# Sixteen heads of eight: 64 rows a head, the maxima inside the score pass, halves through DRAM, and unread matmuls

## The chip, the core and the metric

The kernel runs on one core of a Trainium2 chip. The metric is device microseconds of one execution, as the median of several runs. Engines work from queues of their own: TensorE (PE in the profile, with weight loads under PEld), VectorE (DVE), ScalarE (ACT), GpSimd (POOL) and SyncE (SP), which issues most DMAs.

## The reference

Four transformer layers follow one another on x of shape (16, 256, 128), each with an adaptive layer norm before an attention and before a feed-forward part. Two places matter here. Inside layer 1's feed-forward part there is a full attention with 16 heads of 8 dimensions, and layer 2's attention is a causal one with 16 heads of 8 dimensions and rotary positions:

```python
# layer 1, inner attention
q = (src @ Wq + bq).reshape(B, T, NHEAD, HEAD_DIM)      # NHEAD 16, HEAD_DIM 8, the same for k and v
scores = jnp.einsum('bqhd,bkhd->bhqk', q, k) * scale
probs = jax.nn.softmax(scores, axis=-1)
out = jnp.einsum('bhqk,bkhd->bqhd', probs, v).reshape(B, T, d)
# layer 2, attention
Q, K = rope((x @ qw).reshape(...)), rope((x @ kw).reshape(...))
score = Q @ jnp.swapaxes(K, -1, -2) / jnp.sqrt(jnp.float16(dim))   # masked below the diagonal, softmax
```

T is 256, so each batch row has a 256 x 256 score matrix for each of 16 heads, in both places.

## The kernel before

Activations lie transposed, 128 features on the partitions and 4096 tokens along the free axis, in 8 blocks of 512 tokens (two batch rows each). The stages run one after another: layer 0 attention, layer 0 experts, layer 1 attention, layer 1 inner attention (**stage A** here), layer 1 experts, layer 2 attention (**stage B**), layer 2 experts, layer 3. Stages A and B both run `attend8`, with `spaces8` for their buffers.

**Operands.** q and k are each split into a high and a low part (`parts8`), so that four products high-high, high-low, low-high, low-low add up to the score. `spread8` lays them out by 16 DMAs a block, from SBUF to SBUF: each head gets 32 partition rows (8 dimensions x 4 products), four heads fill 128 partitions, and four such groups c lie side by side. One matmul with 32 rows then gives one head's scores. A stage has 16 units of work, one for each batch row; two units make a block.

**Two passes over the scores.** The first pass computes scores with queries on the partitions, and DVE reduces them to row maxima (L1394). The second pass computes them again with keys on the partitions, subtracts the maxima in the same accumulation by an extra matmul (`pick8` times `mT`, the maxima split into two parts and transposed), and ACT takes the exponential (L1399). `less_maxima` makes `mT`. In stage B a mask is added in the first pass by two bf16 matmuls (`ident16` times `below`), and POOL clears the upper triangle after the exponential (L1402).

**Cycles.** A unit has 8 cycles. A cycle holds four first-pass matmuls of one unit and, `LEAD` + 8 = 10 cycles behind, the eight second-pass matmuls (four scores, four maxima) of an earlier tile; they are interleaved in the order of `steps[0] + steps[1]`. First-pass scores go to `ps_max` and second-pass ones to `ps_exp`, one buffer of two banks each. After them come the things put off from the cycle before (`held`): the maxima's transposes, the values, and `weighted`, which multiplies the exponentials by the values in four column groups of 32. Generators (`sides`, `ready`, `self.later`) add one step each per cycle: the norm and projection of the next block, leaving transposes, output projection, gates. TensorE's instructions keep the program's order (`strict`); other engines' are ordered by a scheduler.

```python
first = [(c, t, j0) for t in range(2) for c in range(2) for j0 in (2, 0)]
...
for o, lhsT, rhs, fresh in steps[0] + steps[1]:
    self.mm(o, lhsT, rhs, start=fresh, skip_group_check=True)
```

Of the kernel before, what the change touches and what calls it, by code (L numbers as in the profile page):

```python
# [20 lines left out]
P = 128  # L21
B, T = 16, 256
NT = B * T
BLK = 512
# [24 lines left out]
def _constants():  # L49
# [19 lines left out]
    put("pick", ((i[:, None] % 32 < 8) & (i[:, None] % 4 == np.arange(4)[None, :])).astype(np.float32))  # L69
# [154 lines left out]
class _Kernel:  # L224
# [825 lines left out]
    def layer1_attn(self):  # L1050
# [4 lines left out]
        with ExitStack() as ctx:  # L1055
# [67 lines left out]
            self.wi = self.load("i1_w", self.w, tag="small")  # L1123

            def inner():
# [4 lines left out]
                self.first_parts = self.w.tile([P, 2, 2, BLK], F32R, tag="m3", name="first_parts")  # L1130
                for _ in self.projected8(self.wi, hb, self.first_parts):
                    yield True

# [37 lines left out]
    LEAD = 2  # L1171

    def spaces8(self, pool, nt, ctx):
# [8 lines left out]
        for n in range(2):  # L1182
# [38 lines left out]
    def spread8(self, parts):  # L1221

        out = self.att.tile([P, 2, 4, BLK], F32R, tag="q8", name="q8")
        src = parts.bitcast(F32).rearrange("p a h t -> p (a h) t")
        for s in range(4):
            of_q, of_k = s // 2, 2 + s % 2
            for c in range(4):
                self.nc.sync.dma_start(
                    out=out.bitcast(F32)[s::4, :, c, :],
                    in_=src[32 * c : 32 * c + 32, of_q : of_k + 1 : of_k - of_q, :],  # L1230
                )
        return [out[:, a] for a in range(2)]

    def unit8(self, qk, hb, at, tok, wv, bias):
        q, k = (x[:, :, tok] for x in qk)
        self.units8.append(dict(q=q, k=k, hb=hb[:, tok], wv=wv, dst=at[:, tok], bias=bias, whole=(hb, at)))

    def attend8(self, group, prepare, finish, scale, causal=False, qmask=None):
# [6 lines left out]
        first = [(c, t, j0) for t in range(2) for c in range(2) for j0 in (2, 0)]  # L1245
# [955 lines left out]
```

## Time and profile before

| what | value |
|---|---|
| median of 6 runs (lowest, highest) | 3223.69 us (3217.08, 3239.49) |
| the profiled execution: its own time, its span | 3231.36 us, 3229.7 us |
| mean granted TensorE clock | 0.899 |
| busy: PE, PEld, DVE, ACT, POOL | 2847.5, 1820.6, 1920.3, 1701.4, 1331.0 us |
| stage A, first maxima matmul to last exponential | 1662.8 to 2049.1 us |
| stage B, the same | 2261.4 to 2730.8 us |
| first-pass reduction L1394 (246 from `ps_max`) | mean 1088 ns |
| exponential L1399 (256) | mean 915 ns |
| `spread8` DMAs | 256 of 128 KB |

The span is the time from the first to the last instruction of the profiled execution. The granted clock is the share of TensorE's clock that was let through. PE's busy time includes time in which matmuls wait in the pipeline, so it is not a measure of how full the array is.

### The profile page before, as it was taken

The page shows a single profiled execution, that of the slowest core. Times are in us where ns is not written, and L with a number is a line of the kernel's source. Part 1 is how long each engine was busy: PE and PEld are TensorE (multiplying, and loading weights), DVE is VectorE, ACT ScalarE, POOL GpSimd, SP SyncE. Part 2 cuts the span into 40 slices and gives each one's busy share as a digit, 9 for nine tenths or more (in the row PEclk, how much of TensorE's full clock was granted, in tenths as well). Part 3 has the DMA queues.
Part 4 walks back from the last instruction along what each step waited for, and adds up shares of the span by engine and source line. Part 5 has one row for each costly group of instructions (what it writes and reads, how often), then busy time and mean ns, then how long its engine had stood idle before and what let it go on. Part 6 is the DMA issues. An engine that isn't in the chain of part 4 may idle for free. (4 is left out here: it accounts for less than half of the span.)

```text
span 3229.7 us, 53104 instructions
## 1 busy us (share of the span) xinstructions
PE 2847.5 (88%) x19238; PEld 1820.6 (56%) x19238; DVE 1920.3 (59%) x4639; ACT 1701.4 (53%) x4484; POOL 1331.0 (41%) x1168
## 2 busy tenths in 40 slices
PE   6999999888979999999969999866789899999777
PEld 3566656555966677776644455564445555555433
DVE  4777777786535666666656666312555563645564
ACT  3777676565435566666625554433243433665533
POOL 4766777772134534443320012233432321333455
PEclk9999999999989999999978877778677776999998
DMA  8050000001752000000021122264212120000000
GB/s 301 2 53 1 9 6 6 11 19 48 225 151 65 14 3 1 1 1 1 1 53 43 43 61 66 71 178 111 51 47 52 27 53 1 1 1 1 4 11 13
DMA packets 87349, 146.14 MB, mean 45 GB/s; under 512 B 14240, under 2 KB 43104, under 8 KB 86832
## 3 DMA queue, kind: packets, MB, share of 16 engines
q1 hardware_dynamic: 65328, 112.98, 13.1%
q0 software_dynamic: 8512, 17.71, 1.9%
q10 hardware_dynamic: 13248, 12.06, 1.1%
q8 instruction: 153, 2.51, 0.3%
q14 instruction: 108, 0.88, 0.1%
HBM read 69.79 MB, written 43.54 MB: 35 GB/s over the span
## 5 line engine op out<-in xcount | busy, mean ns | idle before, releaser
L216 POOL TENSOR_TENSOR E<-E,sm_inv 128x1024 f32<-128x1024 f32 (+1 forms) x241 | 408.0, 1693 | 404.1 <-PE ps_big L259 173.1
L1399 ACT ACTIVATE E<-ps_exp 128x1024 f32<-128x1024 f32 (+1 forms) x256 | 234.2, 915 | 276.6 <-PE ps_exp L259 257.7
L1394 DVE TENSOR_REDUCE m<-ps_max 128x4 f32<-128x1024 f32 (+1 forms) x246 | 267.6, 1088 | 170.3 <-PE ps_max L259 165.4
L216 ACT ACTIVATE E<-E,sm_neg 128x256 f32<-128x256 f32 x512 | 254.1, 497 | 211.8 <-DVE sm_neg L1093 205.0
L216 POOL DMA_INDIRECT rows<-list_rows,l_i x128 | 128.2, 1001 | 497.3 <-ACT list_rows L216 309.7
L262 PEld LDWEIGHTS ps_one<-w_cst,E 128*128 128x128 f32 x1792 | 205.4, 142 | 174.9 <-POOL E L216 98.7
L262 PE MATMUL ps_one<-w_cst,E 128*128 128x128 f32 x1792 | 246.0, 277 | 53.4 <-POOL E L216 35.9
L216 DVE COPY PT<-ps_one 128x512 f32<-128x512 f32 x320 | 209.0, 685 | 96.6 <-PE ps_one L262 94.3
L259 PE MATMUL ps_big<-kT,qT 64*128 64x256 f32 (+1 forms) x2048 | 265.5, 378 | 0.0
L259 PE MATMUL ps_one<-PT,v 128*64 128x256 f32 (+1 forms) x2048 | 225.0, 362 | 3.0 <-DVE PT L216 2.7
L216 ACT ACTIVATE E<-ps_big,sm_neg 128x128 f32<-128x128 f32 (+1 forms) x512 | 208.9, 423 | 25.4 <-DVE sm_inv L216 19.8
L216 POOL TENSOR_TENSOR r_r<-r_r,r_t 128x512 f32<-128x512 f32 x128 | 162.7, 1271 | 137.5 <-DVE r_t L216 120.6
L259 PE MATMUL ps_exp<-q 32*128 32x256 f32 (+1 forms) x1064 | 199.3, 388 | 20.7 <-ACT E L1399 17.5
L1093 DVE CUSTOM_DVE_ANT_0 E<-ps_big,bias 128x256 f32<-128x256 f32 x512 | 186.7, 421 | 51.1 <-PE ps_big L259 24.5
L259 PE MATMUL ps_max<-q 32*128 32x256 f32 (+1 forms) x984 | 158.4, 396 | 51.5 <-DVE m L1394 25.6
L259 PEld LDWEIGHTS ps_big<-kT,qT 64*128 64x128 f32 x2048 | 166.7, 187 | 58.2 <-issue 49.5
L216 POOL DMA_INDIRECT list_rows<-done,origin x128 | 123.2, 963 | 182.5 <-DVE acc L216 41.7
L259 PE MATMUL ps_out<-E,v 128*32 128x256 f32 (+1 forms) x2048 | 191.1, 451 | 3.1 <-POOL E L1402 2.8
L259 PEld LDWEIGHTS ps_max<-q 32*128 32x128 f32 x984 | 97.7, 234 | 150.2 <-issue 73.1
L1402 POOL TENSOR_SCALAR_AFFINE_SELECT E<-E 128x512 f32<-128x512 f32 x128 | 83.0, 650 | 234.5 <-ACT E L1399 234.5
L259 PEld LDWEIGHTS ps_one<-PT,v 128*64 128x64 f32 x2048 | 132.5, 138 | 80.4 <-DVE sm_inv L216 13.6
L259 PE MATMUL ps_exp<-mT,pick 32*128 32x256 f32 (+1 forms) x1024 | 163.4, 329 | 0.0
(351 smaller groups left out, 6460.1 us busy)
## 6 DMA issues: line engine op xcount, KB each, us to landing
q<-parts SPq DMA_DIRECT2D x240, 128.0 KB
rows<-zeros SPq DMA_DIRECT2D x8, 2048.0 KB
list_w<-in_f_W SPq DMA_DIRECT2D x46, 257.0 KB
done<-l_o ACTq DMA_DIRECT2D x92, 128.0 KB
f_W<-in_f_W SPq DMA_DIRECT2D x27, 386.0 KB
f_room<-in_f_W SPq DMA_DIRECT2D x19, 386.0 KB
list_sums<-rows SPq DMA_DIRECT2D x46, 128.0 KB
rb_rows<-rb_d SPq DMA_DIRECT2D x1, 4088.0 KB
```

Source lines behind the costliest of these rows:

```text
L216: ins = f(*args, **kw)
L259: self.ordered(self.nc.tensor.matmul(out, lhsT, rhs, start=start, stop=stop, **kw))
L262: self.ordered(self.nc.tensor.transpose(out, in_, self.c("ident")))
L1093: nc.vector.tensor_tensor_reduce(e[:, i], S[:, i], bias[g][:, i, off : off + T], 1.0, BIG, ALU.add, ALU.min, neg[:, i : i + 1])
L1394: nc.vector.tensor_reduce(o, Sm[:, :, :, :nk], AX.X, ALU.max, negate=True)
L1399: nc.scalar.activation(E, Se[:, :, :, q0:], AF.Exp, scale=scale)
L1402: nc.gpsimd.affine_select(D, D, [[0, 4], [1, P]], ALU.is_ge, 0.0, base=0, channel_multiplier=-1)
```

## The change

- **64 rows a head.** `spread8` gives each head 64 partition rows: row 64 h + 8 d + s for dimension d and product s = 0 to 3. Rows with s = 4 to 7 are zero in q; in k the rows 62 and 63 of each head are one (constant `last`). Two heads fill the partitions and eight groups lie side by side. First-pass matmuls read 60 rows, second-pass ones 64.
- **The maxima in the score pass.** The negated maxima, high and low part, are written by four small DMAs a unit into rows 62 and 63 of q, so the second pass needs no extra matmul. A cycle has 8 score matmuls in place of 12, all of the first pass ahead of the second.
- **Halves through DRAM.** The parts are stored to DRAM by one DMA a block (`stored8`), and each unit is spread from there by 8 DMAs into one of three standing buffers (`q8`, initialised in `spaces8` by DVE, POOL and ACT), called when the unit before the unit before begins its second pass.
- **Unread matmuls.** `turning` issues bf16 matmuls of the identity with itself, 512 columns each, whose result nothing reads: 20 where each stage begins, 2 in each cycle before the second pass has begun, and, in stage A alone, one in each cycle, into the `ps_exp` buffer ahead of the second-pass scores.
- `LEAD` becomes 3, and `weighted` runs for each cycle's own tile, one cycle after it.

```diff
-    put("pick", ((i[:, None] % 32 < 8) & (i[:, None] % 4 == np.arange(4)[None, :])).astype(np.float32))
+    put("last", (i[:, None] % 64 >= 62).astype(np.float32))
...
-    LEAD = 2
+    LEAD = 3
...
             self.v8.append(v)
-            m = pool.tile([P, nt, 4, 4], F32, tag=f"m8_{n}", name=f"m8_{n}")
-            r = pool.tile([P, nt, 4, 32], F32R, tag=f"r8_{n}", name=f"r8_{n}")
-            nc.vector.tensor_copy(r, bc(self.zero.unsqueeze(2).unsqueeze(3), [P, nt, 4, 32]))
+            m = pool.tile([P, nt, 2, 8], F32, tag=f"m8_{n}", name=f"m8_{n}")
+            r = pool.tile([P, nt, 2, 16], F32R, tag=f"r8_{n}", name=f"r8_{n}")
             self.m8.append((m, r))
-        self.pick8 = pool.tile([P, 4, P], F32R, tag="pick8", name="pick8")
-        nc.vector.tensor_copy(self.pick8, bc(self.c("pick").unsqueeze(2), [P, 4, P]))
+        self.q8 = []
+        for n in range(3):
+            q = pool.tile([P, 2, 8, nt * P], F32R, tag=f"q8_{n}", name=f"q8_{n}")
+            shape = [P, 8, nt * P]
+            (nc.gpsimd if n else nc.vector).tensor_copy(q[:, 0], bc(self.zero.unsqueeze(2), shape))
+            nc.scalar.copy(q[:, 1], bc(self.c("last").unsqueeze(2), shape))
+            self.q8.append(q)
...
-    def spread8(self, parts):
-
-        out = self.att.tile([P, 2, 4, BLK], F32R, tag="q8", name="q8")
-        src = parts.bitcast(F32).rearrange("p a h t -> p (a h) t")
+    def stored8(self, parts):
+
+        out = self.parts8_dram.tile([P, 4, BLK], F32, tag="parts", name="parts8")
+        self.nc.sync.dma_start(out=out, in_=parts.bitcast(F32).rearrange("p a h t -> p (a h) t"))
+        return out
+
+    def turning(self, ps, n):
+
+        for _ in range(n):
+            self.mm(ps, self.ident16, bc(self.ident16.unsqueeze(1), [P, 4, P]), skip_group_check=True)
+
+    def spread8(self, u):
+
+        d = self.units8[u]
+        parts, tok = d["parts"]
+        out = self.q8[u % 3]
+        src = parts.rearrange("(c r) x t -> r c x t", r=16)
         for s in range(4):
-            of_q, of_k = s // 2, 2 + s % 2
-            for c in range(4):
-                self.nc.sync.dma_start(
-                    out=out.bitcast(F32)[s::4, :, c, :],
-                    in_=src[32 * c : 32 * c + 32, of_q : of_k + 1 : of_k - of_q, :],
-                )
-        return [out[:, a] for a in range(2)]
-
-    def unit8(self, qk, hb, at, tok, wv, bias):
-        q, k = (x[:, :, tok] for x in qk)
-        self.units8.append(dict(q=q, k=k, hb=hb[:, tok], wv=wv, dst=at[:, tok], bias=bias, whole=(hb, at)))
+            for a, of in enumerate((s // 2, 2 + s % 2)):
+                self.nc.sync.dma_start(out=out.bitcast(F32)[s::8, a], in_=src[:, :, of, tok])
+        d["q"], d["k"] = out[:, 0], out[:, 1]
+
+    def unit8(self, parts, hb, at, tok, wv, bias):
+        self.units8.append(dict(parts=(parts, tok), hb=hb[:, tok], wv=wv, dst=at[:, tok], bias=bias, whole=(hb, at)))
...
         NQ = nt * P
-        first = [(c, t, j0) for t in range(2) for c in range(2) for j0 in (2, 0)]
+        first = [(c, t) for t in range(2) for c in range(4)]
         if causal:
-            then = [(c, t, j0) for t in (1, 0) for c in range(2) for j0 in (0, 2)]
+            then = [(c, t) for t in (1, 0) for c in range(4)]
         else:
-            then = [(c, t, j0) for c in range(2) for t in range(2) for j0 in (0, 2)]
+            then = [(c, t) for c in range(4) for t in range(2)]
...
@@ -1265,23 +1279,31 @@
             while step(g):
                 pass
+        def spread(u):
+            if u % group == 0 and u // group in ready:
+                run(ready.pop(u // group))
+            self.spread8(u)
+
         def start_unit(u):
             blk, i = divmod(u, group)
-            if i == 0:
-                run(ready.pop(blk))
-                if blk + 1 < NBLK:
-                    ready[blk + 1] = prepare(blk + 1)
+            if i == 0 and blk + 1 < NBLK:
+                ready[blk + 1] = prepare(blk + 1)
         def less_maxima(u):
             m, r = self.m8[u % 2]
-            hi = r[:, :, :, :4]
+            hi = r[:, :, 0]
+            m = m.rearrange("p t j c -> p t (j c)")
             nc.vector.tensor_copy(hi, m)
-            nc.vector.tensor_sub(r[:, :, :, 4:8], m, hi.bitcast(F32))
-            ps = self.bank()[:, :NQ]
+            nc.vector.tensor_sub(r[:, :, 1], m, hi.bitcast(F32))
+            ps = self.bank()[:32, :NQ]
             for t in range(nt):
-                self.turned(ps[:, t * P : (t + 1) * P], r[:, t].bitcast(F32).rearrange("p j x -> p (j x)"))
-            mT = U[u]["mT"] = self.att.tile([P, NQ], F32R, tag="mT", name="mT")
+                self.turned(ps[:, t * P : (t + 1) * P], r[:, t].bitcast(F32).rearrange("p s x -> p (s x)"))
+            mT = self.att.tile([32, NQ], F32, tag="mT", name="mT")
             nc.vector.tensor_copy(mT, ps)
+            q = U[u]["q"].bitcast(F32)
+            for n in range(4):
+                row = 64 * (n % 2) + 62 + n // 2
+                nc.sync.dma_start(out=q[row : row + 1], in_=mT[8 * n : 8 * n + 8, :])
...
-        def weighted(u, x, E, i):
+        def weighted(u, x, E):
             d = U[u]
-            c, t, _ = then[x]
+            C, t = then[x]
+            c, i = divmod(C, 2)
             q0 = t * P if causal else 0
-            if i == 0 and t == then[0][1]:
+            fresh = t == then[0][1] and i == 0
+            if fresh:
                 out = self.ps_out.tile([P, 512], F32, tag="out", name="ps_out")
                 d["out", c] = out.rearrange("p (i q) -> p i q", i=2)
             out = d["out", c]
             for j in range(4):
                 self.mm(
                     out[32 * j : 32 * j + 32, i, q0:],
-                    self.v8[u % 2][:, t, 8 * c + 4 * i + j, :],
-                    E[:, j, i, q0:],
-                    start=t == then[0][1] and i == 0,
+                    self.v8[u % 2][:, t, 4 * C + j, :],
+                    E[:, j % 2, j // 2, q0:],
+                    start=fresh,
                     stop=t == then[-1][1],
                     skip_group_check=True,
                 )
             if i == 0:
-
-                held.append(lambda: weighted(u, x, E, 1))
                 return
...
             if mx == 0:
+                run(ready.pop(0))
+                spread(0)
                 start_unit(0)
-            steps = [[], []]
+                spread(1)
+                self.turning(self.ps_out.tile([P, 512], F32, tag="out", name="ps_out"), 20)
+            if live_e and et == 0 and eu + 2 < units:
+                spread(eu + 2)
             if live_m:
-                c, t, j0 = first[mt]
+                c, t = first[mt]
                 nk = (t + 1) * P if causal else NQ
                 d = U[mu]
                 if live_e or mx % 2 == 0:
@@ -1366,39 +1393,38 @@
                 else:
                     Sm = self.ps_exp.tile([P, 1024], F32, tag="exp", name="ps_exp")
-                Sm = Sm.rearrange("p (j i k) -> p j i k", j=2, i=2)
+                Sm = Sm.rearrange("p (r n k) -> p r n k", r=2, n=2)
+                if not live_e:
+                    self.turning(self.ps_out.tile([P, 512], F32, tag="out", name="ps_out"), 2)
                 if qmask is not None:
-                    for j in range(2):
-                        self.mm(Sm[:, j, :, nk - P : nk], self.ident16, bc(qmask.unsqueeze(1), [P, 2, P]), skip_group_check=True)
-                for i in range(2):
-                    for j in range(2):
-                        r = slice(32 * (j0 + j), 32 * (j0 + j) + 32)
-                        q, k = d["q"][r, 2 * c + i, t * P : (t + 1) * P], d["k"][r, 2 * c + i, :nk]
-                        steps[i].append((Sm[:, j, i, :nk], q, k, qmask is None and i == 0))
+                    for r in range(2):
+                        self.mm(Sm[:, r, :, nk - P : nk], self.ident16, bc(qmask.unsqueeze(1), [P, 2, P]), skip_group_check=True)
+                for n in range(2):
+                    for r in range(2):
+                        rows = slice(64 * r, 64 * r + 60)
+                        q, k = d["q"][rows, 2 * c + n, t * P : (t + 1) * P], d["k"][rows, 2 * c + n, :nk]
+                        self.mm(Sm[:, r, n, :nk], q, k, start=qmask is None and n == 0, skip_group_check=True)
             if live_e:
-                xc, xt, xj0 = then[et]
+                xc, xt = then[et]
                 q0 = xt * P if causal else 0
                 e = U[eu]
-                Se = self.ps_exp.tile([P, 1024], F32, tag="exp", name="ps_exp").rearrange("p (j i q) -> p j i q", j=2, i=2)
-                for i in range(2):
-                    rows = [slice(32 * (xj0 + j), 32 * (xj0 + j) + 32) for j in range(2)]
-                    for j, r in enumerate(rows):
-                        k, q = e["k"][r, 2 * xc + i, xt * P : (xt + 1) * P], e["q"][r, 2 * xc + i, q0:]
-                        steps[i].append((Se[:, j, i, q0:], k, q, i == 0))
-                    for j, r in enumerate(rows):
-                        steps[i].append((Se[:, j, i, q0:], self.pick8[r, 2 * xc + i, :], e["mT"][r, q0:], False))
-            for o, lhsT, rhs, fresh in steps[0] + steps[1]:
-                self.mm(o, lhsT, rhs, start=fresh, skip_group_check=True)
+                Se = self.ps_exp.tile([P, 1024], F32, tag="exp", name="ps_exp")
+                if qmask is None:
+                    self.turning(Se[:, :512], 1)
+                Se = Se.rearrange("p (r n q) -> p r n q", r=2, n=2)
+                for n in range(2):
+                    for r in range(2):
...
+                        self.mm(Se[:, r, n, q0:], k, q, start=n == 0, skip_group_check=True)
             if live_m:
-                o = self.m8[mu % 2][0][:, t, j0 : j0 + 2, 2 * c : 2 * c + 2]
+                o = self.m8[mu % 2][0][:, t, :, 2 * c : 2 * c + 2]
                 nc.vector.tensor_reduce(o, Sm[:, :, :, :nk], AX.X, ALU.max, negate=True)
             if live_e:
-                if xj0 == 0:
-                    e["E"] = self.att.tile([P, 4, 2, NQ], F32, tag="E8", name="E8", bufs=3)
-                E = e["E"][:, xj0 : xj0 + 2, :, q0:]
-                nc.scalar.activation(E, Se[:, :, :, q0:], AF.Exp, scale=scale)
+                E = self.att.tile([P, 2, 2, NQ], F32, tag="E8", name="E8", bufs=3)
+                nc.scalar.activation(E[:, :, :, q0:], Se[:, :, :, q0:], AF.Exp, scale=scale)
                 if causal:
-                    D = e["E"][:, xj0 : xj0 + 2, :, q0 : q0 + P].rearrange("p j i q -> p (j i) q")
+                    D = E[:, :, :, q0 : q0 + P].rearrange("p r n q -> p (r n) q")
                     nc.gpsimd.affine_select(D, D, [[0, 4], [1, P]], ALU.is_ge, 0.0, base=0, channel_multiplier=-1)
             now, held = held, []
             for f in now:
@@ -1407,8 +1433,8 @@
                 held.append(lambda u=mu: less_maxima(u))
             if live_e and et == 0:
                 held.append(lambda u=eu: values(u))
-            if live_e and xj0 == 2:
-                held.append(lambda u=eu, x=et, E=e["E"]: weighted(u, x, E, 0))
+            if live_e:
+                held.append(lambda u=eu, x=et, E=E: weighted(u, x, E))
             sides = [g for g in sides if step(g)]
```

More of the change, by code (lines that the diff above doesn't have):

```diff
@@ L1123, in layer1_attn @@
             self.wi = self.load("i1_w", self.w, tag="small")
+            self.parts8_dram = self.pool("parts8", 3, DRAM)
             def inner():
@@ L1129, in inner @@
                     yield True
-                self.first_parts = self.w.tile([P, 2, 2, BLK], F32R, tag="m3", name="first_parts")
-                for _ in self.projected8(self.wi, hb, self.first_parts):
+                parts = self.w.tile([P, 2, 2, BLK], F32R, tag="m3", name="first_parts")
+                for _ in self.projected8(self.wi, hb, parts):
                     yield True
+                self.first_parts = self.stored8(parts)
             D[0] = {}
@@ L1390, in attend8 @@
-            for o, lhsT, rhs, fresh in steps[0] + steps[1]:
-                self.mm(o, lhsT, rhs, start=fresh, skip_group_check=True)
+                Se = self.ps_exp.tile([P, 1024], F32, tag="exp", name="ps_exp")
[4 more added lines that the diff above has]
+                    for r in range(2):
+                        rows = slice(64 * r, 64 * r + 64)
+                        k, q = e["k"][rows, 2 * xc + n, xt * P : (xt + 1) * P], e["q"][rows, 2 * xc + n, q0:]
+                        self.mm(Se[:, r, n, q0:], k, q, start=n == 0, skip_group_check=True)
@@ L1495, in prepare @@
                         yield from self.projected8(wi, hb, parts)
+                        parts = self.stored8(parts)
                     else:
                         hb, parts = self.h1, self.first_parts
-                    qk = self.spread8(parts)
-                    yield
                     at = two.tile([P, BLK], F32, tag="at", name="at", bufs=3)
                     for i in range(2):
-                        self.unit8(qk, hb, at, slice(i * T, (i + 1) * T), wi[:, 2 * P : 3 * P], self.v("i1_bv"))
+                        self.unit8(parts, hb, at, slice(i * T, (i + 1) * T), wi[:, 2 * P : 3 * P], self.v("i1_bv"))
                 def finish(blk, hb, at):
@@ L1701, in prepare @@
                 yield from self.turned8(w, hb, parts)
-                qk = self.spread8(parts)
-                yield
+                parts = self.stored8(parts)
                 at = two.tile([P, BLK], F32, tag="at", name="at", bufs=3)
                 for i in range(2):
-                    self.unit8(qk, hb, at, slice(i * T, (i + 1) * T), w[:, 4 * P : 5 * P], None)
+                    self.unit8(parts, hb, at, slice(i * T, (i + 1) * T), w[:, 4 * P : 5 * P], None)
             def finish(blk, hb, at):
```

## The prediction

> **What bounds the kernel now.** I read the page, then windows cut at the stages, then single 3.41-us stretches, then the timeline of one cycle and of the two stage starts. The page:
>
> ```profile
> span 3229.7 us, 53104 instructions
> PE 2847.5 (88%) x19238; PEld 1820.6 (56%) x19238; DVE 1920.3 (59%) x4639; ACT 1701.4 (53%) x4484; POOL 1331.0 (41%) x1168
> PEclk9999999999989999999978877778677776999998
> ```
>
> The granted clock sags from stage A to the end of stage B, and hardly elsewhere. The windows (busy of PE, PEld, DVE, ACT, POOL, then granted clock) are A's start, A's steady part, what lies between, B's start, B's steady part:
>
> ```profile
> 1662.80:1686.90 24.10, 14.50 (x56) 5.99 (x56) 15.82 (x19) 3.32 (x5) 0.00 (x0) 0.50 0.20 50
> 1686.90:2049.10 362.20, 332.05 (x2974) 184.23 (x2976) 230.25 (x445) 194.69 (x270) 46.90 (x48) 0.79 0.20 52
> 2049.10:2246.60 197.50, 145.37 (x784) 118.05 (x781) 53.38 (x160) 70.16 (x163) 61.59 (x68) 0.79 0.48 136
> 2246.60:2293.60 47.00, 27.91 (x110) 14.25 (x109) 19.32 (x34) 6.84 (x11) 16.97 (x16) 0.64 0.27 68
> 2293.60:2730.80 437.20, 390.94 (x3222) 223.28 (x3222) 235.99 (x447) 170.78 (x279) 133.69 (x172) 0.74 0.15 39
> ```
>
> PE is busy over 89% of both steady parts, no other engine over 64%. At full clock a plain cycle repeats in 1.85 us, paced by the reduction (1.22) and the exponential (1.02) taking turns with PE; at half clock it takes 2.34, paced by PE.
>
> ```profile
> 1708.54 1.22 DVE L1394 TENSOR_REDUCE m<-ps_max 128x4 f32<-128x1024 f32 x1 [1.06 <-PE ps_max L259]
> 1708.81 1.02 ACT L1399 ACTIVATE E<-ps_exp 128x1024 f32<-128x1024 f32 x1 [0.89 <-PE ps_exp L259]
> ```
>
> So the question is what sets the clock. It changes only at boundaries 3.41 us apart, and a busy PE does not bring it back:
>
> ```profile
> 1899.89:1903.30 3.41, 2.57 (x27) 1.31 (x24) 2.70 (x4) 1.35 (x2) 0.00 (x0) 0.50 0.02 5
> 1903.30:1906.71 3.41, 3.41 (x32) 2.29 (x32) 1.38 (x2) 1.02 (x1) 0.00 (x0) 0.50 0.68 160
> 1906.71:1910.13 3.42, 3.42 (x26) 2.06 (x24) 1.32 (x2) 2.04 (x4) 0.00 (x0) 0.50 0.78 195
> ```
>
> What fits is the amount of array streamed. For every matmul I counted its columns times the share of the 128 x 128 array that it uses, over each stretch. At full clock 58 of 61 stretches under 3000 such columns are followed by half clock, and 1 of 664 at 3000 or more; at half clock 53 of 59 at 3000 or more are followed by full clock, and 6 of 127 under it. [...]
>
> **What the change does to that count.** Before, a cycle of A streams 12 x 256 x 1/4 = 768 columns of scores and maxima and 1024 of `weighted`: 1792. After, 8 x 256 x 1/2 = 1024, 512 of turning, 1024: 2560. B gets no turning; its mean cycle goes from 1856 to 2048. I put these weights on the trace's own timing. Of A's stretches, 10 of 62 at full and 32 of 44 at half clock are under 3000 now; after, none and 5. Of B's, 16 of 60 and 51 of 68 now; after, 13 and 30. A should hold full clock; B should in part.
>
> **Stage A, steady (362).** Adding the full-clock period of each of the 16 cycle places in a block (1.84 to 5.02 us) gives 39.6 us; eight blocks are 317, with 8 of the experts' list work that rides along, 325: -37. Against it: matmul pairs start 0.11 us apart, and a cycle loses two pairs (-0.22) but gains a turning (512 columns at the 0.11 us per 256, +0.21) and two changes between full-array and part-array matmuls. Before shows such a change at B's mask:
>
> ```profile
> 2445.93 0.38 PE L259 MATMUL ps_max<-half_below,ident 128*128 128x256 bf16 x2
> 2446.24 0.33 PE L259 MATMUL ps_max<-q 32*128 32x128 f32 x2
> ```
>
> The second bf16 matmul starts 0.11 after the first, the next kind 0.20 after that: 0.09 a change. Net +0.17 a cycle. Nine places are plain ones paced by DVE and ACT, whose waits hide it; the other seven pay: 0.17 x 7 x 8 = +10. [...]
>
> **Starts.** A's 16 DMAs (10.5 us of issue) are followed by the first maxima:
>
> ```profile
> 1651.91 10.54 SPq L1228 DMA_DIRECT2D q<-first_parts  x16
> 1662.82 0.58 PE L259 MATMUL ps_max<-q 32*128 32x256 f32 x2 [11.05 <-DMA q<-first_parts]
> ```
>
> After, the parts were stored earlier, in the experts' time, so only 8 DMAs (8 x 0.65 + 2.2 landing = 7.4) stand ahead of the first unit, but three `q8` buffers are filled first: DVE 2.3, ACT 1.9 each (by 0.69 for 512 and 1.02 for 1024 elements). POOL fills two halves, 5.1 each by its 1.27 for 512, needed only by units 1 and 2. -1 (-5 to +4). The 20 turnings run in this gap and hide, 20 x 0.43 at half clock = 8.5 of 11 us. A's lead, 24.1 us at 0.50, becomes 11 cycles at the faster rate: -3 (-6 to +2). In B the store is new on the path: parts are ready at 2252.3; a 1 MB store lands about 5.5 later by this trace's stores, then 7.4 of spreads: 2265 against 2261.4, +4 (+2 to +8). B's turnings come as soon as `ident16` is there, near 2247, so the clock has fallen again: lead -1 (-5 to +4). Filling B's buffers falls into A's drain, where ACT copies `at`: +1.
>
> **Stage B, steady (437).** Full-clock periods add up to 45.2 a block, 372 in all with the blocks' tail work: -65 if the clock were always full. The count says that half-clock stretches go from 68 to about 25, because the 13 that still fall each last near two: -40 (-65 to 0). The score slot of a cycle shortens with two pairs gone, 0.57 to 0.43 in causal sizes, in the 7 PE-paced places: -8. `weighted` now takes each cycle's own exponential after POOL's clearing (650 ns, 127 in B), where every second one had a cycle more; `held` puts it one cycle later, so a cycle of 1.85 covers 0.65 unless POOL is in a 1.27-us `rot` or `parts` step (24 of them). Before, PE waited for it only 7.6 us. +6 (0 to +20).
>
> **Late maxima.** Rows 62 and 63 now come by DMA: transposes and copies 2.3 us, four issues on SP at 0.33 to 0.65, landing 2.2: 5.8 to 7.1 us after the unit's last reduction is under way. Three cycles of LEAD give 3 x 1.85 + 0.45 = 6.0 in A's odd units, 7 in B's, 10 and more in even ones. On SP they stand behind up to 8 spreads (5.2) and the store, which is itself queued until its parts are complete; whoever waits is the second pass, and behind it in PE's order the first pass and `weighted` of every later cycle. SP has 16 spreads, 8 row DMAs and a store a block, 12.9 us of issue against 30 and more. A: +6 (0 to +12). B: +2 (0 to +8).
>
> **Sum.** A: -1 - 3 - 37 + 10 + 6 = -25. B: +4 - 1 - 40 - 8 + 6 + 2 = -37. Elsewhere +1. Together -61. The profiled execution took 3231.4 (span 3229.7 and 1.7 around it), 7.7 above the median of 3223.7: 3170.4 there, 3163 as a median.
>
> **The rivals.**
> *Only A gains.* B gets no turning, and if its stretches stay under 3000, because faster stretches are also emptier in the 3.6 to 5.4 us cycles, the -40 goes: -25 + 3 + 1 = -21, 3203. For it: 13 full stretches still fall by my count. Against: 51 low half stretches become 30. Chance 0.22.
>
> *Slower: the clock does not follow.* The monitor may not weigh 64-row or unread matmuls as I do; no row before has either. Then A stays near 0.79, and turning is pure cost: +0.17 in seven of 16 places at full (75 cycles, +6), +0.35 in each of 52 half-clock cycles (+18), lead +5, late maxima +6, start -1: +34; B +3, elsewhere +1: +38, 3262. It decides if A's steady clock stays under 0.85. Against: the bf16 mask matmuls and the transposes are counted by the same rule and fit it. Chance 0.14.
>
> *Late maxima.* If the row DMAs land 1.5 us later than I take, because they queue behind the spreads, every unit of 32 stalls that much more: +47, 3210. For: SP's order. Against: 10 us of slack in even units. Chance 0.10.
>
> **How the numbers follow.** The forecast has 0.54. Its own range: low end with B's clock following wholly (-25), POOL and late maxima free (-14) and the starts at half of their better ends (-2), 3122; high end with B's clock gain halved (+20), the late maxima at +18 (+10) and POOL at +20 (+14), 3207. Reaching up to take in the first and third rivals, the range is 3122 to 3218; outside it lie the slower case and a few per cent. This kernel's measurement can tell about 0.3%, 9.7 us, from no change: faster means under 3214. Forecast 0.53, first rival 0.19 and third 0.06 give 0.78; slower 0.15, from the second rival and an edge of the third; 0.07 between.
>
> **What would show it.** Right: PEclk digits of 9 in A's slices and 8 or 9 in B's; A's steady window near 341 us at a clock over 0.95; the exponential's idle time still ended by PE `ps_exp`; few waits of PE on `q<-mT`. Wrong: A's clock under 0.85 (the monitor), B's near 0.74 (only A gains), or PE idle before `ps_exp` ended by a DMA from `mT`, 1.5 us a unit (late maxima). B's first maxima far past 2265 less A's gain would make the start the mis-sized term.

## The result and the profile after

The changed kernel takes 3254.7 us (median of 20 runs, 3232.3 to 3272.8) against 3225.3 for the kernel before on the same chips: ratio 1.0086, interval 1.0070 to 1.0103. It is slower, where the prediction said 3163 and faster. A second series on one chip gave 1.0069 (1.0045 to 1.0092). Whole times differ by up to 2% between chips (before took 3160 to 3229 us in the four series below), so kernels are compared by their ratio to before.

The page of the changed kernel:

```profile
span 3248.5 us, 51876 instructions
PE 2839.6 (87%) x18426; PEld 1786.9 (55%) x18426; DVE 1924.7 (59%) x4635; ACT 1710.2 (53%) x4490; POOL 1337.9 (41%) x1172
PEclk9999999999989999999989998688788978999998
```

The clock did rise: nines reach into stage A, and stage B has more eights. The time did not follow. Windows of A and B, each from its first to its last exponential (busy of PE, PEld, DVE, ACT, POOL, then granted clock):

```profile
1696.40:2091.94 395.54, 354.63 (x2584) 174.33 (x2582) 228.28 (x443) 193.65 (x270) 46.60 (x48) 0.89 0.21 67
2337.29:2750.29 413.00, 342.94 (x2710) 189.91 (x2710) 238.24 (x443) 170.39 (x279) 133.28 (x171) 0.83 0.18 59
```

Cut the same way, before has 361.0 us at 0.79 and 437.1 at 0.74. The difference of the two profiled spans, +18.8, is made of: up to A's first reduction +5.8, A's lead +2.5, A +34.5, from A to B -1.1, B's lead +1.9, B -24.1, the rest -0.7. So B gave 24 of the 40 us forecast from its first exponential on, and A went the wrong way at a higher clock. The same kernel profiled on another chip (e5 below) has A at 391.0 and B at 424.1, so one profile gives A to some 5 us and B to some 11.

I measured a cycle as the time from one first-pass reduction to the next, took for each of a block's 16 places the median over cycles at full clock, and added the 16. That **full-clock block** of A is 40.1 us before (the prediction had 39.6) and 45.5 after: at the same clock a block takes 5.4 us more. (Six of the 16 places of before rest on only one or two cycles at full clock.) One costly cycle and two long stalls show where the time went.

*The costly cycle.* Place 12 of a block (4.04 us, before 1.92):

```profile
1882.38 0.50 PE L259 MATMUL ps_max<-q 60*128 60x256 f32 x4
1883.12 0.58 ACT L1341 COPY oT<-ps_out 128x512 f32<-128x512 f32 x1
1883.27 0.38 PE L259 MATMUL ps_exp<-ident 128*128 128x512 bf16 x1 [0.39 <-ACT E L1425]
1883.58 0.50 PE L259 MATMUL ps_exp<-q 64*128 64x256 f32 x4
1884.01 0.71 PE L259 MATMUL ps_one<-w_i_w,hb 128*128 128x128 f32 x4
1884.18 1.02 ACT L1425 ACTIVATE E<-ps_exp 128x1024 f32<-128x1024 f32 x1 [0.48 <-PE ps_exp L259]
1885.10 0.43 ACT L1314 COPY v<-ps_one 128x128 f32<-128x128 f32 x2
1885.41 0.42 PE L259 MATMUL ps_out<-E,v 128*32 128x256 f32 x4 [0.69 <-ACT v L1314]
```

The turning stands between the two score passes and waits 0.39 us for the exponential's buffer; the second run of scores starts 0.31 after it and takes 0.43 to the next matmul, where the prediction had two pairs of score matmuls at 0.11 each. Then `weighted` waits 0.69 for `v`, which ACT copies only after the exponential.

*One long stall in A's last block.* The maxima's rows were ready at 1996.7, and SP issued them at 2009.9:

```profile
1996.30 0.40 DVE L1302 COPY mT<-ps_one 32x256 f32<-32x256 f32 x1
2003.44 0.36 SPq L1598 DMA_DIRECT2D list_sums<-rows  x1
2004.43 0.35 SPq L1600 DMA_DIRECT2D list_w<-in_f_W  x1
...
2009.49 0.33 SPq L1600 DMA_DIRECT2D list_w<-in_f_W  x1
2009.92 2.83 SPq L1306 DMA_DIRECT2D q<-mT  x4
2013.50 1.38 PE L259 MATMUL ps_exp<-q 64*128 64x256 f32 x4 [9.99 <-DMA q<-mT]
```

Eight list DMAs of the next stage's experts, not ready until 2003.4, stand ahead of them in SP's order. After the stall the clock is half for 58 us, from 2007.6 to 2065.6: a plain cycle at half clock takes 3.00 us, and 2560 columns in 3.00 us are 2910 in a stretch of 3.41, under the 3000 of the prediction's count (in this profile 3 of 74 half-clock stretches under it are followed by full clock, and 50 of 56 at or above it). In e5 the same stall is followed by 20 us at half clock, which ends in cycles that carry other work beside.

*One long stall in B.* In block 5 TensorE waits for a reduction that DVE does not get to, as 42 other instructions (the routing chain of `gates2`) stand between two reductions in its order; before never has more than 10 there in B:

```profile
2602.16 0.41 DVE L216 TENSOR_TENSOR g_sc<-comb,gb 128x256 f32<-128x256 f32 x1
...
2617.38 0.42 DVE L216 TENSOR_REDUCE t_at<-t_hot 128x16 f32<-128x256 f32 x1
2617.72 0.68 DVE L1422 TENSOR_REDUCE m<-ps_max 128x4 f32<-128x512 f32 x1
2618.45 0.58 PE L259 MATMUL ps_max<-half_below,ident 128*128 128x256 bf16 x2 [12.73 <-DVE m L1422]
```

### The profile page after: what moved, and what is told of

The parts are those of the page before. It is cut to its first block, busy times and chain, and to the rows that moved or that the text cites. A ratio compares the mean times of both kernels' runs of the same rounds, so it can differ in the third digit from the quotient of the medians.

```text
span 3248.5 us, 51876 instructions
## 1 busy us (share of the span) xinstructions
PE 2839.6 (87%) x18426; PEld 1786.9 (55%) x18426; DVE 1924.7 (59%) x4635; ACT 1710.2 (53%) x4490; POOL 1337.9 (41%) x1172
## 4 chain that ended last, share of the span: by engine, by line
PE 57%; DVE 9%; ACT 6%; issue 5%; POOL 4%; DMA 2%; SPq 1%; another core or an unknown queue 1%; ACTq 0%; POOLq 0%; DVEq 0%
PE ps_one L259 22%; PE ps_big L259 9%; PE ps_out L259 7%; PE ps_one L262 7%; PE ps_hid L259 3%; PE ps_exp L259 3%; PE ps_max L259 3%; ACT E L1425 2%; DVE m L1422 1%; ACT ln_sq L216 1%; POOL E L216 1%; DVE ln_xc L216 1%; PE ps_rope L259 1%; DMA rows<-list_rows,l_i 1%
## 5 line engine op out<-in xcount | busy, mean ns | idle before, releaser
L259 PE MATMUL ps_out<-E,v 128*32 128x256 f32 (+1 forms) x2048 | 168.4, 405 | 34.9 <-ACT v L1314 18.9
L259 PE MATMUL ps_exp<-q 64*128 64x256 f32 (+2 forms) x1064 | 137.4, 335 | 29.3 <-DMA q<-mT 19.0
L216 DVE TENSOR_REDUCE sm_neg<-ps_big 128x4 f32<-128x512 f32 (+1 forms) x128 | 122.2, 955 | 67.3 <-PE ps_big L259 64.4
L259 PE MATMUL ps_rope<-w_a_qkv,hb 128*128 128x512 f32 x256 | 141.3, 638 | 23.0 <-ACT r_sq L216 19.5
L259 PE MATMUL ps_max<-q 60*128 60x256 f32 (+1 forms) x984 | 133.0, 352 | 24.3 <-DMA q<-parts 15.5
```

The lines of the kernel that those rows point to most:

```text
L216: ins = f(*args, **kw)
L259: self.ordered(self.nc.tensor.matmul(out, lhsT, rhs, start=start, stop=stop, **kw))
```

## The experiments

**Theory:** the clock follows the columns as forecast, but A's cycles were made longer by (S) the turning inside the cycle, (V) `weighted` waiting for the values, (Q) SP's order, and B by (D) DVE's order. **Rivals:** the layout itself is slower, or the clock rather than the waits is still what decides.

Results, by series (one chip each):

| run | ratio to before (interval) | A: us at clock | full-clock block | B: us at clock |
|---|---|---|---|---|
| e1 no cycle turning | 0.9939 (0.9911 to 0.9966) | 353.6 at 0.90 | 41.9 | 411.8 at 0.84 |
| e2 no turning at all | 0.9950 (0.9916 to 0.9984) | 365.4 at 0.86 | 42.4 | 410.6 at 0.84 |
| e3 values early | 0.9979 (0.9961 to 0.9997) | 377.4 at 0.91 | 44.5 | 402.5 at 0.86 |
| e4 before, with turnings | 0.9979 (0.9957 to 1.0000) | 351.1 at 0.93 | 43.5 | 424.4 at 0.75 |
| e5 changed again | 1.0069 (1.0045 to 1.0092) | 391.0 at 0.91 | 45.8 | 424.1 at 0.81 |
| e6 rows by ACT | 1.0217 (1.0175 to 1.0259) | 429.3 at 0.82 | - | 420.1 at 0.81 |
| e7 short turning | 1.0190 (1.0155 to 1.0225) | 421.5 at 0.76 | 44.5 | 423.5 at 0.81 |
| e8 three edits | 0.9963 (0.9941 to 0.9985) | 364.8 at 0.87 | - | 407.3 at 0.84 |
| e9 rows first | 1.0015 (0.9992 to 1.0039) | 384.3 at 0.91 | 45.8 | 424.3 at 0.81 |
| e10 chain held | 1.0051 (1.0031 to 1.0070) | 390.3 at 0.91 | 46.3 | 413.8 at 0.81 |
| e11 four edits | 0.9783 (0.9755 to 0.9812) | 319.0 at 0.95 | 40.4 | 389.0 at 0.86 |
| e12 e11 with cycle turning | 0.9878 (0.9853 to 0.9902) | 353.5 at 0.96 | 44.5 | 396.2 at 0.85 |
| e13 e11, turning ahead | 0.9799 (0.9768 to 0.9831) | 330.5 at 0.99 | 42.6 | 399.5 at 0.84 |
| e14 e11, no turning at all | 0.9740 (0.9709 to 0.9771) | 318.3 at 0.96 | 40.6 | 390.9 at 0.87 |
| e15 e11, LEAD 2 | 0.9865 (0.9834 to 0.9896) | 337.7 at 0.91 | - | 398.3 at 0.84 |
| e16 e11 again | 0.9792 (0.9758 to 0.9825) | 317.4 at 0.96 | 40.9 | 388.0 at 0.88 |

Series are e1 to e4, e5 to e8, e9 to e12 and e13 to e16. A dash stands where too few cycles of some place ran at full clock.

### First series: which part costs

e1, no turning in A's cycles:

```diff
-                if qmask is None:
-                    self.turning(Se[:, :512], 1)
```

> The changed kernel without the one turning in each of stage A's cycles (the 20 at each start and the 2 per leading cycle stay). Theory S (the turning stands between the two score passes, so the score matmuls come in two runs, each with its own 0.2 us of entry; 0.3 to 0.5 us in each of the 7 places of 16 that TensorE paces): a full-clock block of A falls from 45.1 to about 42, but the columns fall by 512 a cycle, so the granted clock of A's steady part drops from 0.89 to about 0.82; both together, within 10 us of the changed kernel's 3255. Theory V (the wait of `weighted` for the values, behind the exponential on ACT, is what lengthens the cycles): a full-clock block stays at 44 to 45, the clock falls as well, and the time is 10 to 25 us longer, 3265 to 3280.

The block fell to 41.9 as theory S has it, but the clock did not fall: 0.90. I had expected it to, and with it the whole gain to be lost. Without the turning a plain cycle still streams 2048 columns in 1.82 us, 3840 in a stretch, and where the clock has fallen 2048 in 2.16, about 3230 in a stretch, which is still over 3000. The kernel is 0.6% faster than before.

e2, `turning` issues nothing:

> The changed kernel with no turning at all, so 64 rows a head, maxima in the score pass and halves through DRAM alone. If the clock follows the streamed columns, A's leading cycles stay at 0.50 (they were 0.76) and cost 3 to 6 us over the run without the cycle turnings; stage B hardly changes, as its 20 come too early. Theory S: 3250 to 3265; theory V: 3268 to 3285. If the layout itself were a gain, this would be under before's 3224; neither theory expects that.

0.9950: the layout alone is no slower than before, and A's lead ran at 0.64. It cannot be told from e1. The first rival falls.

e3, values one cycle earlier:

```diff
-            if live_e and et == 0:
-                held.append(lambda u=eu: values(u))
+            if (ex + 1) % per == 0 and 0 <= (ex + 1) // per < units:
+                held.append(lambda u=(ex + 1) // per: values(u))
```

> The changed kernel with `values` of a unit issued one cycle earlier (ahead of the unit's second pass), so that ACT's copies of v are done before the first `weighted` of the unit. Theory V: the 31 waits of PE `ps_out` on ACT `v` are gone, places 4 and 12 of a block in A fall from 2.7 and 4.0 us to about 1.9, 20 to 35 us less than the changed kernel: 3220 to 3235. Theory S: the waits are hidden slack, at most 8 us less: 3247 or more.

This wait is among the changed kernel's (engine, line, waited for: total, times, longest us) and is absent in e3:

```profile
PE ps_out L259 <- ACT v L1314: 18.9, 31, 0.7
```

Place 4 fell from 2.73 to 1.82, and 12 from 4.04 to 2.40, while 11 rose from 1.98 to 2.63 since the values' matmuls now stand there. Against the changed kernel's two series the ratio is about 0.9% to 1.1% better, 28 to 34 us, the upper end of what V expected.

e4, before with the turnings alone (20 at each start, 2 a leading cycle, one a cycle of A into `Se` ahead of all scores):

```diff
-                Se = self.ps_exp.tile([P, 1024], F32, tag="exp", name="ps_exp").rearrange("p (j i q) -> p j i q", j=2, i=2)
+                Se = self.ps_exp.tile([P, 1024], F32, tag="exp", name="ps_exp")
+                if qmask is None:
+                    self.turning(Se[:, :512], 1)
+                Se = Se.rearrange("p (j i q) -> p j i q", j=2, i=2)
```

> The kernel before with the turnings alone (20 at each stage's start, 2 per leading cycle, one per cycle of A into the exponential's buffer ahead of the score matmuls), on 32 rows a head with the maxima by matmul. Columns per cycle of A go from 1792 to 2304, so by the count A's clock goes from 0.79 to 0.93 or more; the turning then costs 0.3 us in the 7 TensorE-paced places (+17) against at most -37: 3200 to 3215 if the clock is worth what the prediction gave it. By theory S with 0.5 us a cycle in all places at full clock, the gain is used up: 3225 to 3245.

The clock went from 0.79 to 0.93 and A only from 361.0 to 351.1, since plain places rose from 1.85 to 2.16 us. The prediction let the plain places hide the turning; here each pays 0.31.

### Second series: what makes the turning costly, and a wrong cure

e5, the changed kernel again:

> The changed kernel itself, to stand on the same chip as the variants; kernels are compared by their ratio to before. Theory S (the turning inside each cycle of A is what makes the change lose): about 1.005 to 1.012 times before, against 0.994 without the cycle turnings, and A's steady part near 395 us. If the 42 us between the two in A come from the chip instead, the ratio is 0.995 to 1.0 and A's steady part near 360.

It stays slower than before on another chip, with A at 391.0.

e6, the rows' DMAs issued by ACT (`nc.scalar.dma_start` in place of `nc.sync.dma_start` in `less_maxima`):

> The changed kernel with the four DMAs of each unit's maxima issued by ACT in place of SP. Theory Q (in A's last block they stand on SP behind eight list DMAs of the experts that are not ready, so TensorE waits 10 us on `q<-mT` and then stays at half clock): place 3 of block 7 falls from 13.4 us to about 3, block 7 from 61 to 67 us to about 45, and the whole is 15 to 25 us under the changed kernel on the same chip. Theory L (the rows land late in every unit): every block gains by 1 to 3 us. If the four issues cost ACT more than they save: no more than 5 us under it.

The stall of block 7 did go (13.4 to 1.8 us at place 3), but the kernel became 1.5% slower than e5: ACT itself now waits, and its exponentials with it.

```profile
ACT E L1425 <- DMA q<-mT: 33.6, 13, 5.3
ACT ln_sq L216 <- DMA q<-mT: 36.0, 14, 2.9
```

Place 10 rose from 1.9 to between 3.6 and 5.8 us and A fell back to half clock after it in most blocks. Neither Q nor L expected this; ACT's queue was the wrong cure, and e9 tries Q by another.

e7, the cycle turning cut to 128 columns:

```diff
-                    self.turning(Se[:, :512], 1)
+                    self.mm(Se[:, :128], self.ident16, self.ident16, skip_group_check=True)
```

> The changed kernel with A's cycle turning cut from 512 to 128 columns. Theory S says that the turning costs by the entries that it forces (two score runs, each with a first weight load in the open), not by its columns: 0.16 us less array time in each cycle, yet a full-clock block still sums to 44 or more (45.5 with 512 columns, 41.9 without), and the time is within 12 us of the changed kernel. If its columns are the cost, a block sums to about 43 and the time is 20 us or more below.

With a quarter of the columns the full-clock block keeps 44.5 of 45.8 us, as S expects (in the costly cycle above the first weight load of the second score run begins behind the turning, at 1883.57, and its first matmul at 1883.58). But the kernel is not within 12 us of the changed one, it is 1.2% slower: it pays for the place and no longer has the columns, and the clock in A falls to 0.76. A plain cycle at half clock takes 2.68 us here and streams 2176 columns, about 2770 in a stretch, under 3000. About 58 of A's stretches are at half clock, against 21 in e5.

```profile
1693.52:2115.01 421.49, 377.46 (x2584) 196.25 (x2582) 228.78 (x443) 194.52 (x270) 47.33 (x48) 0.76 0.19 63
```

e8, the edits of e1, e3 and e6 together:

> Three edits together: no turning in the cycles of A, the values one cycle earlier, the maxima's rows issued by ACT. If the three causes are apart from one another, A's steady part is 330 to 340 us (354 without the cycle turnings, less 12 in block 7, less 1 to 2 a block at places 4 and 12), B's 400 to 405, and the ratio to before 0.983 to 0.990. B's long place (17 to 20 us at place 7 of block 5, where DVE runs 36 to 43 other instructions between two reductions, 10 at most in before's stage B) is still there.

0.9963: e6's edit spoils it (18.2 us at place 2 of block 7). The estimate of 0.983 to 0.990 counted e6's edit as a gain.

### Third series: the orders of SP and DVE, and all together

e9, the experts' list loads pinned behind whatever SP has been given before them:

```diff
-            row = self.piece_value(half, 0, k, 8 * HALF - PIECE)
+            row = self.pinned_behind(lambda: self.piece_value(half, 0, k, 8 * HALF - PIECE))
```

> The changed kernel with the experts' first list DMAs (and the loads of their addresses) put behind all of stage A's DMAs in SP's order, so that no row DMA of the maxima stands behind a list that is not ready. Theory Q: place 3 of block 7 falls from 13.4 us to about 3 and the clock stays full there; block 7 falls from 62 to 67 us to 46 to 50, and the time is 12 to 20 us under the changed kernel (ratio to before 1.001 to 1.004). Rival: the wait passes to something else in block 7 (the lists' own start after A), and less than 6 us are gained.

Place 3 of block 7 fell from 13.4 to 2.3 us and the ratio to 1.0015. Theory Q holds for the stall, but not for the clock, which Q expected to stay full there: it fell at place 9 of that block and stayed half for 27 us, and A's clock is 0.91 with and without the stall.

e10, the steps of `gates2`, from the fifth on, held to program order (on DVE, ACT and POOL), which leaves at most 14 other instructions between two of B's reductions:

```diff
-                self.later.append(self.gates2(blk))
+                self.later.append(self.pinned(self.gates2(blk)))
```

> The changed kernel with the instructions of `gates2` (the routing chain of stage B's blocks 3 and 7) held to program order, so that DVE runs at most 14 other instructions between two of stage B's reductions, where the changed kernel runs 42 at once. Theory D (the order on DVE, and not the new layout, makes the place of 17 to 20 us in block 5): that place falls to 4 to 6 us, B's steady part from 413 to 424 down by 10 to 18 us, ratio 1.002 to 1.005. Rival: the chain costs the same spread over cycles; B's steady part moves by less than 5 us.

The long place fell from 19.6 to 4.7 us and B to 413.8, against 424 in e5 and e9; the ratio of 1.0051 is at the edge of what D expected, and its interval overlaps e5's. But the changed kernel's first profile has 413.0 in B with the stall in it, so this fall lies within the spread of single profiles. The place is settled, the size in the whole time is not.

e11, the edits of e1, e3, e9 and e10:

> Four edits of the changed kernel: no turning in A's cycles, the values a cycle earlier, the list DMAs behind A's, the routing chain held. If the four causes add up: A's steady part 325 to 338 us, B's 385 to 395, ratio to before 0.975 to 0.983. If the clock falls again where the cycle turning is gone, A's part is 345 to 355 and the ratio 0.984 to 0.99.

0.9783, faster than both kernels, with A even below the expected 325:

```profile
1692.39:2011.35 318.96, 274.34 (x2458) 149.36 (x2458) 227.60 (x443) 192.39 (x270) 47.12 (x47) 0.95 0.24 78
2261.41:2650.43 389.02, 337.07 (x2710) 184.87 (x2710) 228.53 (x443) 170.19 (x279) 132.23 (x171) 0.86 0.19 63
```

From the changed kernel's mean of 1.0078 this is 2.95%. Alone, the four gave about 1.4% (e1), 1.0% (e3), 0.6% (e9) and 0.3% (e10), 3.3% in sum: nearly apart from one another.

e12, the same with the turning back in A's cycles:

> The same without the first edit, so with the turning in A's cycles. Theory S: a full-clock block of A is 3 to 4 us longer than in the run without it and the clock is no better than a few hundredths, so A's steady part is 20 to 30 us longer and the ratio 0.982 to 0.992. If the turning pays once the stalls are gone (full clock throughout A), the two are within 8 us of one another.

A is 34.5 us longer at a clock 0.01 higher, a little over what S expected:

```profile
1694.08:2047.61 353.53, 333.80 (x2585) 164.85 (x2585) 227.94 (x443) 193.19 (x270) 46.77 (x48) 0.96 0.22 70
```

### Fourth series: what was still open

e13, the four edits with a turning ahead of both passes:

```diff
+                if live_e and qmask is None:
+                    self.turning(Sm[:, :, :, :].rearrange("p r n k -> p (r n k)")[:, :512], 1)
```

> The four edits, but with a turning of 512 columns in each cycle of A, put ahead of the first pass and into the maxima's buffer, so that the two score passes follow one another as one run. Theory S (the cost is the second run of scores, not the columns): a full-clock block sums to 41 to 42.5, against 44.5 with the turning between the passes and 40.4 without it; A's steady part 325 to 338 us. If the turning costs its columns and its two changes wherever it stands, the block is at 44 or more and A's part 345 or more.

The block is 42.6, between e16's 40.9 and e12's 44.5. Plain places go from 1.82 to 2.13 (0.31 for the columns and the changes, as in e4), while places 0, 2, 6, 11, 12, 13 and 15 are 0.28 to 0.85 shorter than in e12 (place 5 is 0.43 longer). So of e12's cost about half comes from the columns and changes and half from the place between the passes; S was half of it. The clock was the highest of all, 0.99, and A is 13 us longer than in e16. With e12 this refutes the second rival: the highest clock does not make the shortest A.

```profile
1657.18:1987.68 330.50, 292.90 (x2574) 151.97 (x2574) 228.98 (x443) 192.42 (x270) 46.95 (x48) 0.99 0.23 75
```

e14, the four edits with no turning at all:

> The four edits without any turning, those at the start and in the lead included. If the clock follows the streamed columns, A's lead begins at half clock (0.5 to 0.65 against 0.81 to 0.92) and takes up to 3 us more, and the first block starts at half clock, 2 to 6 us more; all else is the same. Ratio to before 0.978 to 0.983. If the starts' turnings do nothing: within 3 us of the four edits.

0.9740, the lowest ratio:

```profile
1659.49:1977.75 318.26, 273.34 (x2458) 148.84 (x2458) 227.22 (x443) 192.34 (x270) 46.23 (x47) 0.96 0.24 78
2198.64:2589.55 390.91, 337.06 (x2710) 184.18 (x2710) 228.53 (x443) 170.28 (x279) 131.82 (x171) 0.87 0.19 63
```

A's lead ran at 0.72 against 0.93 in e16 and took the same time (23.7 and 23.6 us). The intervals of e14 and e16 overlap, so it is not shown that the starts' turnings cost anything, but nothing shows that they bring anything.

e15, the four edits with `LEAD = 2`:

> The four edits with LEAD at 2. By the prediction's chain (rows landing 5.8 to 7.1 us after a unit's last pass, two cycles of cover being 4.1 us in A's odd units), TensorE waits 1.7 to 3 us on `q<-mT` in odd units of A and up to 2 in B's: 15 to 35 us more than the four edits, less one leading cycle a stage (4 us). If the rows land earlier than that, it is 0 to 5 us faster.

0.7% slower than e16, 24 us, and the wait is the one named; e11 has 7.4 us of it in 12 waits:

```profile
PE ps_exp L259 <- DMA q<-mT: 36.3, 35, 3.6
```

e16, the four edits again:

> The four edits again, as the measure for the three runs beside it: ratio to before 0.975 to 0.982, A's steady part 317 to 325 us, B's 385 to 395.

As in e11.

## Why the prediction was wrong

**The count of columns: right.** In it a column of an f32 matmul other than a score counts twice (in before's trace 128 of them start 0.11 us apart, `ps_out<-f_room,s` at 814.58, as 256 bf16 columns of B's mask do at 2445.93), which the prediction did not say; so the eight `weighted` records of a cycle, 256 columns on a quarter of the array, make its 1024. The count was made on before's trace and holds on the changed kernel's, with 64-row and unread matmuls in it: at full clock 53 of 56 stretches under 3000 columns are followed by half clock, and 1 of 725 at 3000 or more; at half clock 50 of 56 at 3000 or more are followed by full clock, and 3 of 74 under it. The slower rival, a clock that does not follow, is refuted; that the time lies near its 3262 is chance, as its condition, a clock in A under 0.85, was not met (0.89). The "monitor" of that rival is the prediction's word for whatever sets the clock; the profiles show the granted clock alone. The clock does not go with TensorE's busy share: A's TensorE is busy 377 of 421 us in e7 at a clock of 0.76, and 274 of 319 in e11 at 0.95: less busy by the profile, and more clock. Matmuls take longer at half clock (four first-pass ones 0.79 us at 2030.63, against 0.50 at 1882.38), which raises the busy share, so the better evidence is the prediction's stretches that are busy throughout and stay at 0.50.

**The term of -37: failed in its premise.** It took the full-clock cycles of before (39.6 a block) as those of the changed kernel. They became 45.5. A gained the clock (44 half stretches became 24) and spent it. This is the step that turned the forecast around: A was to go from 362 to 341 us, and took 395.5.

**The term of +10 for the turning: mis-sized.** e12 against e11 has +34.5 us in A. The step gave the turning 0.39 us in a cycle (0.21 for its columns, two changes at 0.09), took off 0.22 for two lost pairs, and let nine plain places hide the rest. In a place that TensorE paces, the turning costs 0.52. This is place 0 of a block in e12 (3.93 us):

```profile
1752.70 0.50 PE L259 MATMUL ps_max<-q 60*128 60x256 f32 x4
1753.13 0.39 PE L259 MATMUL ps_exp<-ident 128*128 128x512 bf16 x1
1753.45 0.51 PE L259 MATMUL ps_exp<-q 64*128 64x256 f32 x4
1753.89 0.42 PE L259 MATMUL ps_out<-E,v 128*32 128x256 f32 x4
```

and in e16, without the cycle turning (3.41 us):

```profile
1704.85 0.50 PE L259 MATMUL ps_max<-q 60*128 60x256 f32 x4
1705.19 0.40 PE L259 MATMUL ps_exp<-q 64*128 64x256 f32 x4
1705.52 0.42 PE L259 MATMUL ps_out<-E,v 128*32 128x256 f32 x4
```

From the first scores to `weighted` it is 1.19 us against 0.67. The turning itself takes 0.32, and two runs of two pairs take 0.87 where one run of four takes 0.67. Nine places of e12 are 0.2 to 0.5 longer than in e16, five of them by 0.52, and the other seven hide nearly all of it. TensorE's waits for the exponential's buffer do not grow (3.3 us in A in e12, 2.8 in e11, 4.0 in e16). Where the turning stands ahead of the scores, e13 and e4 show 0.31 in each plain place. Nor do the two lost pairs show: a block without the cycle turning is 40.4 to 40.9 at its best, against 40.1 before.

**That A needed the turning: the choice behind it was never priced.** The prediction weighed 2560 columns a cycle, and worked out neither the layout without the turning nor a cycle at half clock. e1, e11 and e14 hold 0.90, 0.95 and 0.96 with 2048. At half clock a plain cycle repeats in 3.00 us with the turning (the changed kernel) and in 2.16 without it (e11):

```profile
2030.63 0.79 PE L259 MATMUL ps_max<-q 60*128 60x256 f32 x4
2033.63 0.79 PE L259 MATMUL ps_max<-q 60*128 60x256 f32 x4
```

```profile
1975.72 0.80 PE L259 MATMUL ps_max<-q 60*128 60x256 f32 x4
1977.88 0.79 PE L259 MATMUL ps_max<-q 60*128 60x256 f32 x4
```

By the count these are 2910 and about 3230 columns in a stretch, on either side of 3000. So where the clock has fallen, plain cycles without the turning can bring it back, and those with it cannot. Falls that begin at place 8 or 9 of a block last 3 to 8 stretches with the turning between the passes (e3, e5, e9, e10, e12) and 1 to 3 without a turning in the cycle (e1, e2, e11, e14, e16). The gain in A was in the layout, of which the sum counted only the lost pairs: in e14, with no unread matmul and the edits of e3, e9 and e10, A takes 318.3 us, 42.7 less than before.

**`weighted` after its own cycle: half right.** The wait for POOL was named and came out near its size (PE's own waits 2.8 us before, 11.6 after, +6 forecast). The same step also brings `weighted` up against the values' copies on ACT, which the prediction did not follow: 31 waits, 0.9 to 1.1% of the time by e3.

**Late maxima: the chain right, the queue incomplete.** The chain of 5.8 to 7.1 us needs the third cycle of LEAD (e15). But the list of what the rows stand behind on SP, "up to 8 spreads (5.2) and the store", left out the next stage's list DMAs, which cost one unit 10 us, with half clock after it. The third rival came true for one unit rather than 32.

**DVE's order in B: missing.** No step of the prediction asked what the change does to instructions that it does not touch. The same 42 stand in a row in both profiles of the changed kernel, this one and e5's.

**Stage B: -24 where the terms from its first exponential on gave -40.** Half-clock stretches went from 68 to 40, not 25. In e5 it is -13. With the values early and the chain held it is -48 (e11), so the size was there and was taken back by V and D together; what D alone took is not shown. The full-clock sum of 45.2 behind the -40 could not rest on full-clock cycles alone: four of B's 16 places have no cycle wholly at full clock in before. And the first rival, that only A gains, has it the wrong way round: only B gained.

**Starts.** A's first reduction is 5.8 us later in the profiled run and 5.5 earlier in e5's, on another chip, against a forecast of -1; the term is smaller than the spread of what comes ahead, and is not settled. A's lead, forecast at -3 with its clock, came out at +2.5 at 0.76 against 0.50 (+0.6 in e5); in e14 and e16 it takes the same time at 0.72 and 0.93, so the clock is not what sets it there. B's first reduction came 1.1 earlier after A than before, against +4, and its lead 1.9 longer, against -1.

**What stays open.** Why the scheduler puts the whole chain in a row with the new layout, and what the two orders of e9 and e10 would do to the kernel before, was not tried. How much of the whole time D costs is open too.

## What to carry to other kernels

A higher granted clock is worth only what the cycle's own length leaves: price the cycle after the change, at full clock and at half, place by place, and price the change without its helper too. When a step is moved, read the order of every queue around it, also for work of other stages that the change does not touch; here the one on SP cost 0.6% of the time (e9), and the one on DVE a stall of 12.7 us in one block. The padding matmuls that raised the clock lengthened the cycle too: in A they cost 13 us (e13, 0.99 and 330.5 us, against e16's 0.96 and 317.4) and 34 us (e12, 0.96 and 353.5, against e11's 0.95 and 319.0) more than they brought.

## What the runs showed of the hardware

In stage A a plain cycle could keep the clock low by its own length. That of 2560 columns, with the turning between the passes, takes 1.82 us at full clock, 4800 columns a stretch, and 3.00 us at half, 2910, under the 3000 of the count; falls that begin at place 8 or 9 of a block last 3 to 8 stretches with it. That of 2048 columns takes 1.82 and 2.16, 3840 and about 3230, over 3000; such falls last 1 to 3 with it. Matmuls added to raise the clock thus made it harder to regain.

The runs show time lost where the turning stands between the two score passes. In a cycle that TensorE paces, a turning with 0.21 us of columns there costs 0.52 (1.19 us in e12 against 0.67 in e16), so 0.31 beyond its columns: 0.11 of it in the turning's own 0.32, and 0.20 in the scores, 0.87 in two runs against 0.67 in one. Two changes at the 0.09 of before's row would be 0.18; what passes in TensorE at a change is not shown.
